# Layer 2 of a two-layer kernel: from a scheduler's order to an order laid out by hand

## The chip, the cores and the metric

The kernel runs on one core of one Trainium2 chip. The metric is the device time of one execution in microseconds (us), lower is better. Every number below comes from the times of the kernel before, from the page of its one profiled execution, or from an answer of that execution's trace.

## The reference

An input of 4 images, 192 channels, 128 x 128 pixels, passes through two residual layers, `x = x + layer(GroupNorm(x))`. Layer 1 (fractional and ordinary Fourier transforms) is not touched. Layer 2 is a selective scan over the 16384 pixels of each image, with 384 inner channels and 16 states per channel, all in float32. Cut to what matters:

```python
seq = layernorm_over_channels(groupnorm(x))            # 192 channels
xs, z = split(in_proj_w @ seq)                         # 384 + 384
u = silu(causal_conv4(xs))
dt, B, C = split(x_proj_w @ u, [12, 28])               # 12 + 16 + 16 rows
dt = softplus(dt_proj_w @ dt + b)
# for each pixel t, channel d, state s:
h[d, s] = h[d, s] * exp(dt[d] * A[d, s]) + (dt[d] * u[d]) * B[s]
y[d] = sum_s h[d, s] * C[s] + u[d] * Dp[d]
out = x + out_proj_w @ (y * silu(z))
```

## The kernel before, in words

Layer 1 (`layer0` in the code) ends before layer 2 (`layer1`) begins; the first scan of layer 2 starts at 2670.8 us of the profiled execution. Layer 2 works on chunks of T = 512 pixels, 32 for each image, 128 in all. The inner channels lie on partitions as NJ = 3 tiles of 128; the states go in pairs (G = 2), so a chunk has 3 x 8 = 24 groups, one for each tile j and pair of states.

**The front of a chunk** (`front`, a generator that stops at each `yield`): load `xm` (L557), GroupNorm on DVE (L560), mean over channels by matmuls with ones (L566), subtraction (L568), square on ACT (L572), variance by matmuls (L578), square root on ACT (L583), reciprocal and a diagonal matrix on DVE (L584, L586), its broadcast by matmuls (L589), scaling (L593); then in_proj (L606) to `xs` (L612), the convolution as four matmuls with diagonal matrices (L617), silu to `u` (L620) and, of the other half of in_proj, to `zs` (L622); x_proj (L628), copied to `xd` (L632), whose rows of B and C go to DRAM as `dbc`; dt_proj (L640), softplus to `dt` (L643) and the product `dtu = dt * u` on DVE (L644).

**A group** (`inputs`, `decays`, `scans`): `bc` is a pair's B and C, broadcast from DRAM to all partitions (1 MB per load). `db = dtu * B` is made on DVE from `dp`, a copy of `dtu` in PSUM (L677), or, for one group of three, on POOL from `dtu` itself (L675). ACT makes two `da = exp(dt * A)` in PSUM (L687). DVE runs two scans `h` (L701), ACT copies their last column to `carry` (L705), POOL multiplies `hc = h * C` (L707), PE adds up `hc` in PSUM by matmuls with the identity (L712), and after a tile's last pair adds `u * Dp` (L714). DVE then gates, `yg = py * zs` (L716). `finish` makes out_proj (L727), adds `xm` (L731) and stores. A float32 matmul is two PE instructions in the trace.

**What sets the order.** The groups go in two halves of states, each over the three tiles (`HALVES = 2`). `bc` has 6 buffers of the 8 that a chunk needs, `da` two PSUM banks, `ps` (all of the front's matmuls and `finish`) two, each `py{j}` one of its own, `h` four, `hc` three. The loop at the end of `layer1` asks for `inputs` two groups ahead, `decays` one ahead and a step of the next chunk's `front` at every second group; what is left of it is asked for at group 21. The order in which instructions then stand in each engine's queue is not this one: the tile framework's scheduler lays it out when the program is built. Each engine works through its own queue in that order, and waits on semaphores for the other engines, for DMAs and for buffers to come free.

Of the kernel before, what the change touches and what calls it, by code (L numbers as in the profile page):

```python
# [19 lines left out]
CH = 96  # L20
# [462 lines left out]
def layer1(tc, xmid, out, st2, w, n_tok=S * S):  # L483
# [5 lines left out]
    with ExitStack() as ctx:  # L489
# [7 lines left out]
        fp = pool("l1f", 2)  # L497
        jp = pool("l1j", 5)
        tp = pool("l1t", 2)
        bcp = pool("l1b", 6)  # L500
# [4 lines left out]
        psa = pool("l1a", 2, space=PSUM)  # L505
        psy = pool("l1y", 1, space=PSUM)
# [15 lines left out]
        nc.vector.memset(eps, 1e-5)  # L522

# [22 lines left out]

        last = {}
# [4 lines left out]
        def front(i, got):  # L552

            b, ch = divmod(i, NCHUNK)
            at = slice(ch * T, (ch + 1) * T)
            xm = xp.tile([CH, 2, T], F32, name="xm")
            nc.sync.dma_start(out=xm, in_=xmid[b][:, at].rearrange("(t p) f -> p t f", p=CH))  # L557
            s = lp.tile([CH, 2, T], F32, name="s")
            for t in range(2):
                nc.vector.tensor_scalar(  # L560
                    s[:, t, :], xm[:, t, :], st2[:, b, t, 0:1], st2[:, b, t, 1:2],
                    ALU.subtract, ALU.mult,
                )
            mu = psum()
# [5 lines left out]
            )  # L570
            sq = lp.tile([CH, 2, T], F32, name="sq")
# [4 lines left out]
            for q in range(4):  # L576
                for t in range(2):
                    nc.tensor.matmul(  # L578
                        var[:, q : q + 1], sq[:, t, q * 128 : (q + 1) * 128], ones[0:CH, 0:1],
                        start=t == 0, stop=t == 1,  # L580
                    )
            rs = tp.tile([128, 4], F32, name="rs")
            nc.scalar.activation(rs, var[:, 0:4], AF.Sqrt, bias=eps, scale=1.0 / C)  # L583
            nc.vector.reciprocal(rs, rs)  # L584
            dg = lp.tile([128, 4, 128], F32, name="dg")
            nc.vector.tensor_tensor(dg, _bc(ident, 1, 4), _bc(rs, 2, 128), ALU.mult)  # L586
            rb = psum()
# [6 lines left out]
            xs = fp.tile([128, NJ, T + 3], F32, name="xs")  # L594
            if ch == 0:
                nc.gpsimd.memset(xs[:, :, 0:3], 0.0)
            else:
                nc.gpsimd.tensor_copy(xs[:, :, 0:3], last["xs"][:, :, T : T + 3])
            last["xs"] = xs
            zs = [jp.tile([128, T], F32, name="zs") for _ in range(NJ)]  # L600
            u = [jp.tile([128, T], F32, name="u") for _ in range(NJ)]
# [8 lines left out]

            for j in range(NJ):
                nc.scalar.activation(xs[:, j, 3:], in_proj(j), AF.Identity, bias=bxz[:, j : j + 1])  # L612
            yield
            for j in range(NJ):
                pc = psum()
                for k in range(4):
                    nc.tensor.matmul(  # L617
                        pc, dcw[:, j, k, :], xs[:, j, k : k + T], start=k == 0, stop=k == 3
                    )
                nc.scalar.activation(u[j], pc, AF.Silu, bias=cb[:, j : j + 1])  # L620
            for j in range(NJ):
                nc.scalar.activation(  # L622
                    zs[j], in_proj(NJ + j), AF.Silu, bias=bxz[:, NJ + j : NJ + j + 1]
                )
            yield
            px = psum()
            for j in range(NJ):
                nc.tensor.matmul(  # L628
                    px[0 : RANK + 2 * NS], xpT[:, j, :], u[j], start=j == 0, stop=j == NJ - 1
                )  # L630
            xd = tp.tile([RANK + 2 * NS, T], F32, name="xd")
            nc.scalar.copy(xd, px[0 : RANK + 2 * NS])  # L632
            dbc = dram.tile([2, NS, T], F32, name="dbc")
            nc.sync.dma_start(out=dbc.rearrange("a s t -> (a s) t"), in_=xd[RANK:, :])
            yield
            dt = [jp.tile([128, T], F32, name="dt") for _ in range(NJ)]
            dtu = [jp.tile([128, T], F32, name="dtu") for _ in range(NJ)]
            for j in range(NJ):
# [3 lines left out]
                )  # L642
                nc.scalar.activation(dt[j], pd, AF.Softplus, bias=dtb[:, j : j + 1])  # L643
                nc.vector.tensor_mul(dtu[j], dt[j], u[j])  # L644
            yield
            got.update(xm=xm, zs=zs, u=u, dt=dt, dtu=dtu, dbc=dbc)

        HALVES = 2  # L650
        NG = NS // G // HALVES
        groups = [(hf, j, hf * NG + q) for hf in range(HALVES) for j in range(NJ) for q in range(NG)]
        NGR = len(groups)

        def load_bc(i, got):

            sg = len(got["bc"])
            t = bcp.tile([128, 2, G, T], F32, name="bc")
            nc.sync.dma_start(
                out=t, in_=got["dbc"][:, sg * G : (sg + 1) * G, :].partition_broadcast(128)  # L660
            )
            got["bc"].append(t)

        def inputs(n, k, got):

            hf, j, sg = groups[k]
            if k % NG == 0:
                dp = psd.tile([128, T], F32, name="dp")
                nc.scalar.copy(dp, got["dtu"][j])  # L669
                got["dp"] = dp  # L670
            if sg == len(got["bc"]):
                load_bc(n, got)
            db = scp.tile([128, G, T], F32, name="db")
            if k % 3 == 2:
                nc.gpsimd.tensor_tensor(db, _bc(got["dtu"][j], 1, G), got["bc"][sg][:, 0], ALU.mult)  # L675
            else:
                nc.vector.tensor_tensor(db, _bc(got["dp"], 1, G), got["bc"][sg][:, 0], ALU.mult)  # L677
            got["db", k] = db

        def decays(n, k, got):  # L680

            hf, j, sg = groups[k]
            das = []
            for g in range(G):
                st = sg * G + g
                da = psa.tile([128, T], F32, name="da")
                nc.scalar.activation(da, got["dt"][j], AF.Exp, scale=A[:, j, st : st + 1])  # L687
                das.append(da)
            got["da", k] = das

        def scans(n, k, got):
            hf, j, sg = groups[k]
            ch = n % NCHUNK
            if k == 0:
                got["carry"] = tp.tile([128, NJ, NS], F32, name="carry")
                got["before"], last["carry"] = last.get("carry"), got["carry"]
            db, das = got.pop(("db", k)), got.pop(("da", k))
            h = scp.tile([128, G, T], F32, name="h")
            for g in range(G):
                st = sg * G + g  # L700
                nc.vector.tensor_tensor_scan(  # L701
                    h[:, g, :], das[g], db[:, g, :],
                    0.0 if ch == 0 else got["before"][:, j, st : st + 1], ALU.mult, ALU.add,
                )
            nc.scalar.copy(got["carry"][:, j, sg * G : (sg + 1) * G], h[:, :, T - 1])  # L705
            hc = scp.tile([128, G, T], F32, name="hc", bufs=3)
            nc.gpsimd.tensor_tensor(hc, h, got["bc"][sg][:, 1], ALU.mult)  # L707
            if hf == 0 and k % NG == 0:
                got["py", j] = psy.tile([128, T], F32, name=f"py{j}")
            py = got["py", j]  # L710
            for g in range(G):
                nc.tensor.matmul(py, ident, hc[:, g, :], start=sg == 0 and g == 0, stop=False)  # L712
            if hf == HALVES - 1 and k % NG == NG - 1:
                nc.tensor.matmul(py, ddp[:, j, :], got["u"][j], start=False, stop=True)  # L714
                yg = op.tile([128, T], F32, name="yg", bufs=4)
# [176 lines left out]
```

## Time and profile before

| what | us or share |
|---|---|
| median of 3 runs | 15999.61 (15998.29 to 16002.89) |
| the profiled execution's own time | 15985.05 |
| its span, first to last instruction | 15983.3 |
| PE, busy share of the span | 85% |
| DVE | 78% |
| POOL | 62% |
| ACT | 58% |
| DMA queue of all tensor transfers, share of 16 engines | 27.1% |
| ACT table loads of layer 2, per chunk (L687, L620, L643, L622, L583) | 16 |

The page gives for each engine its busy time, then groups of instructions by line: engine, operation, written tile and read tiles, shapes, count, busy time, mean ns of one, and the engine's idle time just before them with the engine that ended it. Shares of the whole span mix the two layers: layer 2 is about five sixths of it. The time of the profiled execution lies 14.6 us under the median.

### The profile page before, as it was taken

The page shows a single profiled execution, that of the slowest core. Times are in us where ns is not written, and L with a number is a line of the kernel's source. Part 1 is how long each engine was busy: PE and PEld are TensorE (multiplying, and loading weights), DVE is VectorE, ACT ScalarE, POOL GpSimd, SP SyncE. Part 2 cuts the span into 40 slices and gives each one's busy share as a digit, 9 for nine tenths or more (in the row PEclk, how much of TensorE's full clock was granted, in tenths as well). Part 3 has the DMA queues.
Part 4 walks back from the last instruction along what each step waited for, and adds up shares of the span by engine and source line. Part 5 has one row for each costly group of instructions (what it writes and reads, how often), then busy time and mean ns, then how long its engine had stood idle before and what let it go on. Part 6 is the DMA issues. An engine that isn't in the chain of part 4 may idle for free. (4 is left out here: it accounts for less than half of the span.)

```text
span 15983.3 us, 106086 instructions
## 1 busy us (share of the span) xinstructions
PE 13547.5 (85%) x31224; PEld 5507.4 (34%) x31224; DVE 12438.0 (78%) x11315; ACT 9233.8 (58%) x14682; POOL 9838.8 (62%) x4338
## 2 busy tenths in 40 slices
PE   6978978888888888888888888888888888888888
PEld 5342432333333333333333333333333333333333
DVE  5345244888888888888888888888888888888888
ACT  1122123666666666666666666666666666666665
POOL 0000002777777777777777777777777777777777
PEclk8566566999999999999999999999999999999999
DMA  5344322222222222222222222222222222222222
GB/s 154 92 113 115 91 80 81 88 81 93 93 88 93 88 81 92 93 88 93 90 84 87 93 92 89 92 84 85 93 93 88 93 91 81 89 93 88 93 91 76
DMA packets 488164, 1462.09 MB, mean 91 GB/s; under 512 B 63805, under 2 KB 114750, under 8 KB 487070
## 3 DMA queue, kind: packets, MB, share of 16 engines
q1 hardware_dynamic: 474270, 1404.97, 27.1%
q0 software_dynamic: 13312, 50.34, 1.0%
q8 instruction: 246, 4.03, 0.1%
q14 instruction: 336, 2.75, 0.1%
HBM read 1312.45 MB, written 142.74 MB: 91 GB/s over the span
## 5 line engine op out<-in xcount | busy, mean ns | idle before, releaser
L707 POOL TENSOR_TENSOR hc<-h,bc 128x1024 f32<-128x1024 f32 x3072 | 7344.9, 2397 | 3547.8 <-DVE h L701 2869.2
L701 DVE TENSOR_TENSOR_SCAN h<-da,carry,db 128x512 f32<-128x512 f32 x5952 | 7294.2, 1264 | 891.4 <-ACT da L687 891.0
L712 PE MATMUL py<-hc,ident 128*128 128x512 f32 x12288 | 6353.3, 644 | 1768.2 <-POOL hc L707 1767.7
L687 ACT ACTIVATE da<-dt,c_A_log 128x512 f32<-128x512 f32 x6144 | 4216.6, 690 | 3715.3 <-DVE h L701 3658.7
L712 PEld LDWEIGHTS py<-hc,ident 128*128 128x128 f32 x12288 | 2287.4, 199 | 5318.4 <-POOL hc L707 2872.6
L677 DVE TENSOR_TENSOR db<-dp,bc 128x1024 f32<-128x1024 f32 x2048 | 2448.6, 1200 | 393.9 <-DMA bc<-dbc 388.9
L675 POOL TENSOR_TENSOR db<-dtu,bc 128x1024 f32<-128x1024 f32 x1024 | 2450.3, 2393 | 36.4 <-DMA bc<-dbc 36.0
L606 PE MATMUL ps<-s,c_wiT 96*128 96x512 f32 x3072 | 1454.0, 602 | 69.3 <-ACT u L620 48.1
L617 PE MATMUL ps<-xs,dcw 128*128 128x512 f32 x3072 | 1373.9, 596 | 115.8 <-ACT u L620 115.8
L687 ACT ACT_TABLE_LOAD x1018 | 1306.1, 1283 | 16.3
L463 POOL DMA_DIRECT2D xmid<-xt x64 | 40.6, 634 | 1528.4 <-DVE xt L461 1528.4
L606 PEld LDWEIGHTS ps<-s,c_wiT 96*128 96x128 f32 x3072 | 572.5, 193 | 926.8 <-issue 616.2
L617 PEld LDWEIGHTS ps<-xs,dcw 128*128 128x128 f32 x3072 | 571.2, 189 | 897.2 <-issue 676.9
L461 DVE TENSOR_TENSOR xt<-xt,pr 96x1024 f32<-96x1024 f32 x128 | 155.8, 1217 | 784.3 <-PE pr L458 784.3
L727 PE MATMUL ps<-yg,c_woT 128*96 128x512 f32 x1536 | 701.7, 592 | 0.0
L644 DVE TENSOR_TENSOR dtu<-dt,u 128x512 f32<-128x512 f32 x384 | 656.5, 1736 | 35.5 <-ACT dt L643 30.0
L452 ACT COPY x<-ps 16x512 f32<-16x512 f32 x128 | 73.5, 574 | 828.3 <-PE ps L449 828.3
L705 ACT COPY carry<-h 128x2 f32<-128x2 f32 x3072 | 548.3, 178 | 1.5 <-DVE h L701 1.5
L669 ACT COPY dp<-dtu 128x512 f32<-128x512 f32 x768 | 447.3, 582 | 96.0 <-DVE db L677 96.0
L620 ACT ACT_TABLE_LOAD x382 | 490.1, 1283 | 9.4 <-PE ps L617 2.8
L628 PE MATMUL ps<-u,c_xpT 128*44 128x512 f32 x768 | 484.6, 782 | 9.0 <-ACT u L620 9.0
L192 DVE TENSOR_SCALAR xn<-xt,gst 96x1024 f32<-96x1024 f32 x256 | 199.6, 803 | 373.4 <-PE ps L260 330.2
(158 smaller groups left out, 10543.5 us busy)
## 6 DMA issues: line engine op xcount, KB each, us to landing
bc<-dbc SPq DMA_DIRECT2D x1024, 1024.0 KB, 5.5
xt<-in_x SPq DMA_DIRECT2D x192, 768.0 KB, 5.0
xmid<-xt POOLq DMA_DIRECT2D x64, 768.0 KB, 4.7
xm<-xmid SPq DMA_DIRECT2D x128, 384.0 KB, 4.3
out<-o SPq DMA_DIRECT2D x128, 384.0 KB, 3.1
df<-u SPq DMA_DIRECT2D x16, 512.0 KB, 2.7
u<-df SPq DMA_DIRECT2D x16, 512.0 KB, 5.0
dimg<-img SPq DMA_DIRECT2D x4, 2048.0 KB, 9.5
```

What stands on the lines that cost most here:

```text
L606: nc.tensor.matmul(pp, wiT[:, t, m * 128 : (m + 1) * 128], s[:, t, :], start=t == 0, stop=t == 1)
L617: nc.tensor.matmul(pc, dcw[:, j, k, :], xs[:, j, k : k + T], start=k == 0, stop=k == 3)
L620: nc.scalar.activation(u[j], pc, AF.Silu, bias=cb[:, j : j + 1])
L644: nc.vector.tensor_mul(dtu[j], dt[j], u[j])
L675: nc.gpsimd.tensor_tensor(db, _bc(got["dtu"][j], 1, G), got["bc"][sg][:, 0], ALU.mult)
L677: nc.vector.tensor_tensor(db, _bc(got["dp"], 1, G), got["bc"][sg][:, 0], ALU.mult)
L687: nc.scalar.activation(da, got["dt"][j], AF.Exp, scale=A[:, j, st : st + 1])
L701: nc.vector.tensor_tensor_scan(h[:, g, :], das[g], db[:, g, :], 0.0 if ch == 0 else got["before"][:, j, st : st + 1], ALU.mult, ALU.add,)
L705: nc.scalar.copy(got["carry"][:, j, sg * G : (sg + 1) * G], h[:, :, T - 1])
L707: nc.gpsimd.tensor_tensor(hc, h, got["bc"][sg][:, 1], ALU.mult)
L712: nc.tensor.matmul(py, ident, hc[:, g, :], start=sg == 0 and g == 0, stop=False)
L727: nc.tensor.matmul(po[0:CH], woT[:, j, t * CH : (t + 1) * CH], got["yg", j], start=j == 0, stop=j == NJ - 1,)
```

## The change

Only layer 2 changes, in ten points:

1. The whole of it is issued inside `tc.manual_schedule()`: instructions stand in every engine's queue in the order in which the program text issues them.
2. `HALVES` is gone: the groups of a chunk go tile by tile, k = 8 j + (pair of states). `bc` has 8 buffers, so that all B and C of a chunk stay resident; the load of a pair for the next chunk is issued when its buffer's last reader of this chunk has been issued: pairs 0 to 6 in iterations 17 to 23, pair 7 in iteration 0 of the next chunk. `dp` is copied 3 times a chunk, not 6.
3. GroupNorm is two `activation(Identity, scale, bias)` on ACT, with a bias tensor `nmr` made once, in place of two `tensor_scalar` on DVE.
4. Silu and softplus are issued in pairs where two inputs are there: u(0) with u(1), u(2) with z(0), softplus 0 with 1, softplus 2 alone, z(1) with z(2).
5. POOL makes `db` in two groups of five (10 of 24), not one of three (8 of 24).
6. `da` has 3 PSUM banks, not 2; an exponential is issued right after each scan, for the state 3 places on. `py` has 2 banks shared by the three tiles, not one for each.
7. PE's sums for a group are issued one iteration after its scans. The gate of tile j is issued an iteration later still.
8. `front` has 22 steps, not 7 or so, one for each iteration. It starts at iteration 22 of two chunks before: in iteration k stands step k+3 of the next chunk (var in 2, the root in 3, `rs` and `dg` in 4, in_proj 0 to 2 in 7 to 9, conv 0 to 2 in 10 to 12, silu_u(0), silu_u(1) in 12, silu_u(2) and silu_z(0) in 14, `xd` in 15, softplus and `dtu` 0 and 1 in 17, 2 in 18, silu_z(1) and (2) in 19).
9. `finish` is three steps, in iterations 3, 4 and 5 of the next chunk.
10. The last three columns of `xs` go to a tile `halo` of their own, so one `xs` buffer is enough; `h` has 3 buffers, not 4; `xm` is loaded earlier.

In each iteration the text issues: `inputs` two groups ahead, the two scans with an exponential after each, `carry`, `hc`, the sums of the group before, the gate, `finish`, a step of `front`, and loads. The diff, cut to its core:

```diff
-        bcp = pool("l1b", 6)
+        bcp = pool("l1b", NS // G)
-        psa = pool("l1a", 2, space=PSUM)
-        psy = pool("l1y", 1, space=PSUM)
+        psa = pool("l1a", 3, space=PSUM)
+        psy = pool("l1y", 2, space=PSUM)
...
             for t in range(2):
-                nc.vector.tensor_scalar(
-                    s[:, t, :], xm[:, t, :], st2[:, b, t, 0:1], st2[:, b, t, 1:2],
-                    ALU.subtract, ALU.mult,
-                )
+                nc.scalar.activation(
+                    s[:, t, :], xm[:, t, :], AF.Identity,
+                    bias=nmr[:, b, t : t + 1], scale=st2[:, b, t, 1:2],
+                )
...
+            a = conv(0)
+            yield
+            c = conv(1)
+            yield
+            silu_u(0, a)
+            silu_u(1, c)
+            a = conv(2)
+            yield
+            c = in_proj(NJ)
+            yield
+            silu_u(2, a)
+            silu_z(0, c)
             px = psum()
...
+            def softplus(j, pd):
                 nc.scalar.activation(dt[j], pd, AF.Softplus, bias=dtb[:, j : j + 1])
                 nc.vector.tensor_mul(dtu[j], dt[j], u[j])
...
+            a, c = dt_proj(0), dt_proj(1)
+            yield
+            softplus(0, a)
+            softplus(1, c)
+            a = dt_proj(2)
+            yield
+            softplus(2, a)
+            a, c = in_proj(NJ + 1), in_proj(NJ + 2)
+            yield
+            silu_z(1, a)
+            silu_z(2, c)
...
-            if k % 3 == 2:
+            if 2 * k % 5 < 2:
...
+        with tc.manual_schedule():
...
+            for pos, (n, k) in enumerate(order):
+                j, sg = divmod(k, NG)
+                if pos + 2 < len(order):
+                    inputs(*order[pos + 2])
+                scans(pos, n, k)
+                if pos:
+                    sums(*order[pos - 1])
+
+                if sg == 1 and pos > 1:
+                    m, q = order[pos - 2]
+                    gate(m, q // NG)
+                    if q == NGR - 1:
+                        tail = finish(m)
+                if k in (3, 4, 5):
+                    next(tail, None)
+                if k == NGR - 2:
+                    for _ in ahead:
+                        pass
+                    ahead = front(n + 2) if n + 2 < total else iter(())
+                next(ahead, None)
+                if k == NGR - 8 and n + 2 < total:
+                    load_x(n + 2)
+                if k >= NGR - 7 and n + 1 < total:
+                    load_bc(n + 1, k - (NGR - 7))
+                if k == 0 and n:
+                    load_bc(n, NG - 1)
```

`scans` after the change issues, for each of its two states, a scan and then `decay`, the exponential three states on:

```python
            for q in range(G):
                st = sg * G + q
                nc.vector.tensor_tensor_scan(
                    h[:, q, :], das.pop(G * pos + q), db[:, q, :],
                    0.0 if ch == 0 else g["before"][:, j, st : st + 1], ALU.mult, ALU.add,
                )
                decay(G * pos + q + 3)
            nc.scalar.copy(g["carry"][:, j, sg * G : (sg + 1) * G], h[:, :, T - 1])
            hc = scp.tile([128, G, T], F32, name="hc", bufs=3)
            nc.gpsimd.tensor_tensor(hc, h, g["bc", sg][:, 1], ALU.mult)
            g["hc", k] = hc
```

## The prediction

> **What bounds the kernel now.** I read the page first, for the engines and the costliest groups.
>
> ```profile
> span 15983.3 us, 106086 instructions
> ...
> L707 POOL TENSOR_TENSOR hc<-h,bc 128x1024 f32<-128x1024 f32 x3072 | 7344.9, 2397 | 3547.8 <-DVE h L701 2869.2
> L701 DVE TENSOR_TENSOR_SCAN h<-da,carry,db 128x512 f32<-128x512 f32 x5952 | 7294.2, 1264 | 891.4 <-ACT da L687 891.0
> L712 PE MATMUL py<-hc,ident 128*128 128x512 f32 x12288 | 6353.3, 644 | 1768.2 <-POOL hc L707 1767.7
> ...
> L677 DVE TENSOR_TENSOR db<-dp,bc 128x1024 f32<-128x1024 f32 x2048 | 2448.6, 1200 | 393.9 <-DMA bc<-dbc 388.9
> ...
> L628 PE MATMUL ps<-u,c_xpT 128*44 128x512 f32 x768 | 484.6, 782 | 9.0 <-ACT u L620 9.0
> L644 DVE TENSOR_TENSOR dtu<-dt,u 128x512 f32<-128x512 f32 x384 | 656.5, 1736 | 35.5 <-ACT dt L643 30.0
> ```
>
> All of these are layer 2. By the timeline its first scan starts at 2670.8, so a chunk takes (15983.3-2670.8)/128 = 104.0 us. The busy times over that stretch:
>
> ```profile
> 2670.80:15983.30 13312.50, 11343.68 (x25764) 4543.17 (x25764) 11355.22 (x9971) 8726.00 (x13918) 9740.89 (x4222) 0.95 0.26 89
> ```
>
> The columns after the length are PE, PEld, DVE, ACT and POOL: PE and DVE are both busy 85%, POOL 73%, ACT 66%, DMA 26%. No engine is full; DVE idles about 15 us of each chunk. The table of waits, then one chunk's timeline of DVE and of ACT, say where.
>
> ```profile
> DVE h L701 <- ACT da L687: 928.2, 559, 3.4
> DVE db L677 <- DMA bc<-dbc: 388.9, 126, 4.9
> DVE s L593 <- PE ps L589: 356.8, 127, 3.2
> ```
>
> ```profile
> 9066.52 3.62 DVE L701 TENSOR_TENSOR_SCAN h<-da,carry,db 128x512 f32<-128x512 f32 x3
> 9073.81 1.23 DVE L677 TENSOR_TENSOR db<-dp,bc 128x1024 f32<-128x1024 f32 x1 [3.67 <-DMA bc<-dbc]
> ...
> 9081.34 2.46 DVE L701 TENSOR_TENSOR_SCAN h<-da,carry,db 128x512 f32<-128x512 f32 x2 [2.25 <-ACT da L687]
> 9086.05 1.28 DVE L701 TENSOR_TENSOR_SCAN h<-da,carry,db 128x512 f32<-128x512 f32 x1 [2.25 <-ACT da L687]
> ```
>
> ```profile
> 9077.32 1.28 ACT L622 ACT_TABLE_LOAD   x1
> 9078.62 0.69 ACT L622 ACTIVATE zs<-ps,bxz 128x512 f32<-128x512 f32 x1
> 9079.32 1.28 ACT L687 ACT_TABLE_LOAD   x1
> 9080.62 0.69 ACT L687 ACTIVATE da<-dt,c_A_log 128x512 f32<-128x512 f32 x1
> ```
>
> A silu between two exponentials holds the scan for two table loads. PE's timeline gives its rate, warm and cold:
>
> ```profile
> 9062.73 7.03 PE L617 MATMUL ps<-xs,dcw 128*128 128x512 f32 x16
> 9103.71 4.83 PE L628 MATMUL ps<-u,c_xpT 128*44 128x512 f32 x6
> ```
>
> Sixteen take 7.03, so one starts each 0.43 us; the six of L628 need 0.8 each after idle gaps (2.77 for six in the chunk before).
>
> **What the Trainium skill says.** "ScalarE: Activation LUTs", Table sets: functions of different sets need a load at each change. The trace agrees, at 1283 ns. "SBUF — State Buffer", Who interferes with whom: a DVE instruction with two SBUF inputs and a GpSimd one that reads SBUF exclude each other for a whole instruction. The trace agrees: `dtu` takes 1.74 us in the mean where `yg`, as large but with a PSUM input, takes 0.67. "TensorE: Matmul & The Clock Gate", Part 1: the array's clock halves after an idle window of some 3.4 us; L628 above fits.
>
> **The change part by part.** Prices are start to start in the timelines: scan 1.18, DVE `db` 1.12, `hc` 2.33, POOL `db` 2.36, exponential 0.63, table load 1.29, 512-wide PE pass 0.43.
>
> *DVE work.* GroupNorm leaves it: 2 x 1.22 = 2.4 less. POOL makes 10 `db` instead of 8: 2 x 1.12 = 2.2 less. What stays: 48 x 1.18 + 14 x 1.12 = 72.3; the two mean/scale steps, `rs`, `dg`, three gates, two adds 6.1; three `dtu` 2.0 plus 2.3 for one lock by a POOL `db`. Sum **82.7 us**.
> *POOL*: 24 x 2.33 + 10 x 2.36 + 0.4 = 79.9. *PE*, unchanged: 178 passes x 0.43 + 3 for the small ones = 79.5. *ACT*: 12 table loads instead of 16 (-5.1), 3 `dp` copies instead of 6 (-1.7), 2 GroupNorm steps (+1.4, priced as `xs` at 0.68: the same operation on as many columns; the trace has no such step reading SBUF, so 0.6 to 1.1 each, `sq`'s 1.06 for 1024 columns being the top; beside the scans in iteration 22, and 1.4 on the path if ACT has no lead there): 68 becomes 63. DMA: the same eight 1 MB loads; eight buffers put each one 5 groups (16 us) ahead against 5.5 us to landing, so the DMA wait goes (-3 us); In SP's queue the loads stand behind `dbc`'s store (1.6 us to landing) and the `xm` load, neither of which comes late; if they did, 3 us return. POOL's halo copy (0.2) waits for xs(2) of ACT, which is done before `hc` of that iteration. A third `da` bank gives the exponentials one scan more of lead, 1.4 us beyond what they need; silu pairs cost 3.9.
>
> So the three engines lie within 4% of each other and each now runs in a fixed order. What is late next has to be followed by hand. I take the steady chunk from iteration 7 (DVE free at 0, POOL at 3.1) and let each instruction start when its queue and inputs allow:
> - *7 to 12*: PE must do 10 pieces, sums, three in_proj and two conv, 21.5 us without a gap from 3.1; conv(1) ends at 24.6. DVE is through group 12 at 19.3. ACT's table is loaded at 21.4, but silu_u(1) waits for conv(1): silu ends 25.6, table 26.8, two exponentials, carry, and only then the `dp` copy, ending 28.8. DVE's next instruction at 21.6 is db(16), which needs it: **7.2** idle, the largest.
>   DVE's ends of groups 7 to 14 on this clock: 3.5, 5.8, 10.0, 13.4, 15.8, 19.3, 21.6, 32.3.
> - *14 to 16*: silu_u(2) with silu_z(0) holds one exponential: 0.9.
> - *17, 18*: `dtu` stands in DVE's queue before the next scans and waits for softplus behind a table load: 2.3 and 2.9. Behind them in DVE's queue are the next `db` and both scans, so `hc` and ACT's exponentials wait too. Before, scans filled that (0.4 idle at L644). In 18 PE's in_proj for silu_z(2) waits 4.3 for softplus(2) to free its bank, with the next sums behind it; PE has by then caught up, so it costs nothing if `hc` keeps two buffers free, else up to 4.
> - *19 to 22*: silu_z pair: 0.9.
> - *20 to 4*: POOL never pauses (13 instructions, 30.4 us); PE's sums, var and po0 follow it, so gate and the first add wait 0.4 and 2.5.
>
> Idle sum 17.0, near the 15 of before: the DMA and exponential stalls go, the fixed order's come. 82.7 + 17.0 is 99.7; the clock kept by hand closes at 100.2. Clock: L628's excess is 6 x (0.782-0.593) = 1.1 us a chunk; somewhere between 0 and that also falls on PE's chain after, take 0.5. **100.7 us**. Saving 104.0-100.7 = 3.3, x 127 steady chunks = 419 us. Prologue and layer 1 unchanged within 10 us. 15985-419 = 15566 for the profiled execution, which lay 15 below the median: **15580**. Adding a PE latency of 0.15 to every hand-over on the first chain, or losing the lock, moves a chunk by 2 either way: 15330 to 15830.
>
> **The rivals.**
> 1. *The waits are covered and DVE's work is the bound.* If PE's block of 7 to 12 starts earlier, 2.8 of the 7.2 goes, and if POOL's run doesn't hold the adds, 2.9 more; with the lock's 2.3 the chunk is 92.2: 11.8 x 127 = 1500, **14500**. For it: POOL has 20 us of slack a chunk. Against: POOL, PE and DVE must all recover within three `hc` buffers.
> 2. *PE goes cold in the block of 7 to 12.* After idle gaps (iterations 18 to 22 leave some of 3 to 4 us) the pass takes 0.85. The block is on the path, so from 3.3 us more, a pass at 0.50, it is slower than before; with half the block cold, +10.7 to 111.4: +7.4 x 127 + 16000 = **16940**. Against: conv passes run at 0.43 in the trace, and the block is dense.
> 3. *No difference*: the fixed order is not what runs, or idle rises to 20 and eats the saved work: **16000**. Against the first: the built order has 12 table loads a chunk and silu in pairs.
>
> **How the numbers follow.** Forecast 0.72, rival 1 0.11, rival 2 0.12, rival 3 0.05. A difference under 0.2% (32 us) can't be told from none. Faster 0.83, same 0.05, slower 0.12. The range leaves out rival 2's 16940 (0.12) and most of rival 1, and takes in the forecast's bounds, half the road to rival 1 and the case of no change: 15050 to 16010.
>
> **What would show it.** Right: chunk near 100.7; one DVE idle of about 7 us before db(16), put down to ACT's `dp`, whose ACT queue waited for conv; 2 to 3 us before each `dtu`; no wait for `bc`; DVE busy near 82%; POOL without pause in groups 20 to 4. Wrong: the db(16) gap missing (rival 1), or conv passes above 0.5 us (rival 2), or `hc` stopped by PE's sums.

## The result and the profile after

The changed kernel takes **16221.27 us** (median of 4 runs, 16200.8 to 16230.14); the kernel before, beside it on the same chip, 16001.25 (15998.29 to 16023.56). The ratio is 1.0133, 95% interval 1.0115 to 1.015: slower by 1.3%, about 220 us. The forecast was 15580 with a range of 15050 to 16010, so sign and range were both missed.

The profiled execution took 16200.8, its span 16199.0. First the page of the kernel after, with the rows that answer to those of before (line, engine, operation, tiles, count | busy us, mean ns | idle of the engine just before, and what ended it):

```profile
span 16199.0 us, 103417 instructions
...
L756 POOL TENSOR_TENSOR hc<-h,bc 128x1024 f32<-128x1024 f32 x3072 | 7196.7, 2356 | 3359.9 <-DVE h L749 3329.6
L767 PE MATMUL py<-hc,ident 128*128 128x512 f32 x12288 | 6449.1, 653 | 1732.5 <-POOL hc L756 1722.8
L749 DVE TENSOR_TENSOR_SCAN h<-da,carry,db 128x512 f32<-128x512 f32 x5952 | 7220.8, 1261 | 197.7 <-ACT da L736 197.1
...
L723 DVE TENSOR_TENSOR db<-dp,bc 128x1024 f32<-128x1024 f32 x1792 | 2157.3, 1204 | 903.2 <-ACT dp L718 902.3
L622 PE MATMUL ps<-s,c_wiT 96*128 96x512 f32 x3072 | 1687.1, 677 | 384.4 <-ACT dt L689 383.0
L641 PE MATMUL ps<-xs,dcw 128*128 128x512 f32 x3072 | 1381.0, 592 | 0.0
...
L690 DVE TENSOR_TENSOR dtu<-dt,u 128x512 f32<-128x512 f32 x384 | 513.4, 1362 | 671.0 <-ACT dt L689 670.9
...
L587 DVE SCALAR_TENSOR_TENSOR s<-ps,s 96x1024 f32<-96x1024 f32 x128 | 156.2, 1221 | 559.4 <-PE ps L585 559.4
```

The scans' wait for exponentials fell from 891 us to 197, and DVE's wait for `bc` is gone. In their place stand waits that were small or absent: `db` for the `dp` copy (902), `dtu` for softplus (671), and one that the prediction did not have at all: **559 us before the subtraction of the mean (L587), which waits for PE's `mu` matmuls (L585).**

The same stretch of layer 2 after, from 11 us ahead of its first scan on (length, then PE, PEld, DVE, ACT, POOL busy, the granted clock, DMA share, GB/s):

```profile
2660.00:16199.00 13539.00, 11395.08 (x25776) 4680.43 (x25776) 10728.86 (x9466) 8023.76 (x13288) 10160.83 (x4606) 0.93 0.26 88
```

By chunk (divided by 128): DVE works 83.8 us and idles (13539.0 - 10728.9)/128 = 22.0. Before it worked 88.7 and idled 15.3. The change took away 4.9 us of work and put 6.7 us of idle time in. That is 1.8 a chunk, times 127 = 225 us: the whole difference of 220, within the rounding. The table of waits of DVE from 2700 us on (us in total, times, longest) says what the idle time waits for:

```profile
DVE db L723 <- ACT dp L718: 896.0, 128, 7.6
DVE dtu L690 <- ACT dt L689: 644.3, 254, 2.9
DVE s L587 <- PE ps L585: 556.1, 126, 6.1
DVE o L788 <- PE ps L783: 247.3, 127, 3.1
DVE yg L774 <- PE py L769: 229.7, 131, 3.2
DVE h L749 <- ACT da L736: 204.9, 254, 1.0
```

One chunk in DVE's timeline shows them one after the other (start, length, operation, count, and in brackets the idle time before it and what ended it):

```profile
8013.03 1.22 DVE L723 TENSOR_TENSOR db<-dp,bc 128x1024 f32<-128x1024 f32 x1 [7.03 <-ACT dp L718]
...
8022.08 1.28 DVE L749 TENSOR_TENSOR_SCAN h<-da,carry,db 128x512 f32<-128x512 f32 x1 [0.80 <-ACT da L736]
...
8029.72 3.35 DVE L690 TENSOR_TENSOR dtu<-dt,u 128x512 f32<-128x512 f32 x2 [2.21 <-ACT dt L689]
...
8038.30 0.69 DVE L690 TENSOR_TENSOR dtu<-dt,u 128x512 f32<-128x512 f32 x1 [2.87 <-ACT dt L689]
...
8056.10 2.44 DVE L749 TENSOR_TENSOR_SCAN h<-da,carry,db 128x512 f32<-128x512 f32 x2
8063.25 1.22 DVE L587 SCALAR_TENSOR_TENSOR s<-ps,s 96x1024 f32<-96x1024 f32 x1 [4.71 <-PE ps L585]
```

The last two lines are what the forecast lacked. DVE is through its scans at 8058.54 and has more to do, but L587 stands next in its queue. POOL's and PE's timelines of the same time say why `mu` is late:

```profile
8048.45 2.38 POOL L721 TENSOR_TENSOR db<-dtu,bc 128x1024 f32<-128x1024 f32 x1
8050.78 2.36 POOL L756 TENSOR_TENSOR hc<-h,bc 128x1024 f32<-128x1024 f32 x1
8053.08 2.37 POOL L721 TENSOR_TENSOR db<-dtu,bc 128x1024 f32<-128x1024 f32 x1
8055.40 6.97 POOL L756 TENSOR_TENSOR hc<-h,bc 128x1024 f32<-128x1024 f32 x3
```

```profile
8053.19 1.98 PE L767 MATMUL py<-hc,ident 128*128 128x512 f32 x4 [2.67 <-POOL hc L756]
8057.82 3.06 PE L767 MATMUL py<-hc,ident 128*128 128x512 f32 x4 [2.64 <-POOL hc L756]
8060.67 2.54 PE L585 MATMUL ps<-s,ones 96*96 96x512 f32 x4
```

A number in brackets is the group of the chunk: hc(22) is `hc` of group 22. The scans of group 22 end at 8051.5, but POOL is late: it is still in hc(21), which stood behind db(23), and has db(0) of the next chunk to do as well. hc(22), the first of the three in the last line, starts at 8055.40 and ends at 8057.73. PE's sums of group 22 start then; the `mu` matmuls, which need only `s` (made by ACT at 8052.33 to 8053.9), stand behind these sums in PE's queue and end at 8063.2; then DVE goes on. The Trainium skill ("TensorE: Matmul & The Clock Gate", Part 2) says that PE keeps matmuls in program order, and the trace agrees: `mu` was ready to run from 8053.9 on and PE stood idle for 2.64 us before 8057.82, without taking it. That nothing else held `mu` back is what the first experiment shows.

### The profile page after: what moved, and what is told of

It is laid out like the page before. It is cut to its first block, busy times and chain, and to the rows that moved or that the text cites. A ratio compares the mean times of both kernels' runs of the same rounds, so it can differ in the third digit from the quotient of the medians.

```text
span 16199.0 us, 103417 instructions
## 1 busy us (share of the span) xinstructions
PE 13599.8 (84%) x31224; PEld 5647.6 (35%) x31224; DVE 11807.0 (73%) x10804; ACT 8524.8 (53%) x14045; POOL 10258.8 (63%) x4722
## 4 chain that ended last, share of the span: by engine, by line
PE 32%; DVE 29%; issue 15%; POOL 13%; ACT 9%; DMA 1%; POOLq 0%; SPq 0%; DVEq 0%; ACTq 0%
DVE h L749 17%; PE py L767 12%; POOL hc L756 10%; PE ps L641 5%; DVE db L723 5%; PE ps L622 5%; ACT da L736 3%; POOL db L721 3%; DVE dtu L690 3%; PE ps L783 2%; ACT L689 2%; PE ps L585 2%; PE ps L260 1%; DVE dg L608 1%; ACT dt L689 1%
## 5 line engine op out<-in xcount | busy, mean ns | idle before, releaser
L756 POOL TENSOR_TENSOR hc<-h,bc 128x1024 f32<-128x1024 f32 x3072 | 7196.7, 2356 | 3359.9 <-DVE h L749 3329.6
L767 PE MATMUL py<-hc,ident 128*128 128x512 f32 x12288 | 6449.1, 653 | 1732.5 <-POOL hc L756 1722.8
L721 POOL TENSOR_TENSOR db<-dtu,bc 128x1024 f32<-128x1024 f32 x1280 | 3046.2, 2380 | 23.1 <-DMA bc<-dbc 23.1
L723 DVE TENSOR_TENSOR db<-dp,bc 128x1024 f32<-128x1024 f32 x1792 | 2157.3, 1204 | 903.2 <-ACT dp L718 902.3
L622 PE MATMUL ps<-s,c_wiT 96*128 96x512 f32 x3072 | 1687.1, 677 | 384.4 <-ACT dt L689 383.0
L641 PE MATMUL ps<-xs,dcw 128*128 128x512 f32 x3072 | 1381.0, 592 | 0.0
L622 PEld LDWEIGHTS ps<-s,c_wiT 96*128 96x128 f32 x3072 | 662.9, 220 | 1311.5 <-issue 746.9
L690 DVE TENSOR_TENSOR dtu<-dt,u 128x512 f32<-128x512 f32 x384 | 513.4, 1362 | 671.0 <-ACT dt L689 670.9
L641 PEld LDWEIGHTS ps<-xs,dcw 128*128 128x128 f32 x3072 | 581.6, 189 | 736.9 <-issue 736.9
L587 DVE SCALAR_TENSOR_TENSOR s<-ps,s 96x1024 f32<-96x1024 f32 x128 | 156.2, 1221 | 559.4 <-PE ps L585 559.4
L635 ACT ACTIVATE xs<-ps,bxz 128x512 f32<-128x512 f32 x384 | 264.4, 688 | 550.7 <-PE ps L622 475.0
L458 PE MATMUL pr<-cat,c_w2T 48*96 48x512 f32 x512 | 473.6, 1079 | 3.1 <-ACT cat L455 3.1
L449 PE MATMUL ps<-xn,c_w1T 96*16 96x512 f32 x512 | 475.3, 1034 | 0.0
```

Source lines behind the costliest of these rows:

```text
L622: nc.tensor.matmul(pp, wiT[:, t, m * 128 : (m + 1) * 128], s[:, t, :], start=t == 0, stop=t == 1)
L641: nc.tensor.matmul(pc, dcw[:, j, k, :], xs[:, j, k : k + T], start=k == 0, stop=k == 3)
L721: nc.gpsimd.tensor_tensor(db, _bc(g["dtu"][j], 1, G), g["bc", sg][:, 0], ALU.mult)
L723: nc.vector.tensor_tensor(db, _bc(g["dp"], 1, G), g["bc", sg][:, 0], ALU.mult)
L756: nc.gpsimd.tensor_tensor(hc, h, g["bc", sg][:, 1], ALU.mult)
L767: nc.tensor.matmul(py, ident, hc[:, q, :], start=sg == 0 and q == 0, stop=False)
```

## The experiments

My **theory** after the result: the time is lost to the laid-out order itself, by instructions that stand in a queue ahead of work that could go on, and the step that I missed is the one chain POOL `hc` - PE sums - `mu` - DVE. **Rivals**: PE's lower clock after short idle gaps; POOL's two extra `db`; GroupNorm on ACT; or a fault common to any order. Edits are against the changed kernel unless another is named. The middle two columns of this table are us from 2700 us of the profiled execution to 15 us before its end. Gains "a chunk" are differences of medians, divided by 128.

| kernel | median us | DVE busy | DVE idle | ratio to before, 95% |
|---|---|---|---|---|
| after | 16221.27 | 10698 | 2786 | 1.0133 (1.0115-1.015) |
| mu_first | 15931.1 | 10633 | 2622 | 0.9957 (0.9943-0.9972) |
| dp_early | 15835.69 | 10690 | 2432 | 0.9901 (0.9887-0.9916) |
| dtu_late | 15786.8 | 10944 | 2110 | 0.9871 (0.9856-0.9885) |
| three | 14972.03 | 10707 | 1548 | 0.9364 (0.9348-0.9379) |
| free_order | 15570.66 | 11033 | 1829 | 0.9737 (0.9723-0.9752) |
| pool_third | 16396.1 | 10906 | 2757 | 1.0251 (1.0199-1.0303) |
| warm | 16183.07 | 10670 | 2768 | 1.0117 (1.0102-1.0132) |
| norm_dve | 16362.54 | 11242 | 2421 | 1.0222 (1.0208-1.0236) |
| norm_act_alone | 15932.0 | 10993 | 2222 | 0.9951 (0.9939-0.9964) |
| five | 14737.23 | 10822 | 1200 | 0.9214 (0.9199-0.923) |
| six | 14590.55 | 11012 | 857 | 0.9116 (0.9104-0.9129) |
| seven | 14876.47 | 11221 | 946 | 0.9292 (0.9278-0.9306) |
| front_first | 15372.29 | 10648 | 2011 | 0.9603 (0.9587-0.9619) |
| front_gate | 15688.26 | 10862 | 2093 | 0.98 (0.9785-0.9815) |

### mu_first: the `mu` matmuls ahead of the sums, nothing else

```diff
+                if k == NGR - 1:
+                    next(ahead, None)
                 if pos:
                     sums(*order[pos - 1])
...
-                next(ahead, None)
+                if k != NGR - 1:
+                    next(ahead, None)
```

> Edit: in iteration 23 the two mean matmuls (mu, L585) are issued ahead of PE's sums for group 22; nothing else moves. Theory (one late chain: DVE's L587 stands ahead of the scans of the next group and waits for mu, mu stands behind sums(22), sums(22) waits for hc(22), hc(22) stands behind two db on POOL): the wait before L587, 4.4 us a chunk after the change, falls under 1, and 3 to 4 us of it come off the chunk, as POOL stands idle 2.4 and 1.7 us just after it: 105.7 to about 102, 15,750 us. Rival (POOL and PE are full there, so another wait takes its place, at the first add, the gate or the scan's buffer): under 1.5 us a chunk, above 16,030 us.

Measured: 15931.1, 290 us or 2.3 a chunk less than after, between theory and rival. DVE's waits of this kernel:

```profile
DVE o L788 <- PE ps L783: 582.1, 127, 7.5
...
DVE s L587 <- PE ps L585: 0.7, 3, 0.3
```

The wait for `mu` is gone as expected, but the add of the last chunk's output (L788), which waits for out_proj, grew from 247 to 582. out_proj and `var` also stand behind sums in PE's queue, so most of the time won was waited for a little later: the theory holds for this wait, but it is one of several on the same chain. Some 0.7 of the 2.3 is not this wait at all: `dg` (L608) took 909 ns in the mean here, 1621 after the change (more on this at the end).

### dp_early: the third `dp` copied two iterations sooner, ahead of the silu pair

```diff
-            if sg == 0:
-                g["dp"] = psd.tile([128, T], F32, name="dp")
-                nc.scalar.copy(g["dp"], g["dtu"][j])
+            if sg == 0 and k != 2 * NG:
+                copy_dp(n, j)
...
+                if k == 2 * NG - 4:
+                    copy_dp(n, 2)
```

> Edit: the dp copy of the third tile is issued in iteration 12, ahead of the silu pair on ACT, not in 14 behind it. Theory (db(16) waits only because the copy stands behind silu_u(1), which waits for conv(1)): the wait of db(16), 7.05 us a chunk, goes; some 3.5 us of it come back as a wait of the second scan of group 14 for its exponential, which stands behind the same pair; net 3.5 us, 15,780 us. Rival (the whole stall belongs to the silu pair and the copy is only where it shows): the scans wait as long, gain under 1 us a chunk, above 16,090 us.

Measured: 15835.69, 3.0 a chunk less than after; the theory's figure is 56 us away. The wait of 896 before `db` is gone; the scans' wait for exponentials behind the silu pair rose from 205 to 887.8:

```profile
DVE h L752 <- ACT da L739: 887.8, 381, 4.1
```

The silu pair still waits for conv(1), and that now shows at the scans; but DVE and POOL get on with `db` and scans before it, and DVE's whole idle time falls by 354 us. The total fits better than its parts: 5.3 a chunk came back at the scans, not the 3.5 of the theory, and the waits before `dtu` and for `mu` fell by 1.1 and 0.9, which it did not have.

### dtu_late: the product `dtu` one iteration after its softplus

```diff
             def softplus(j, pd):
                 nc.scalar.activation(dt[j], pd, AF.Softplus, bias=dtb[:, j : j + 1])
+
+            def product(j):
                 nc.vector.tensor_mul(dtu[j], dt[j], u[j])
...
             a = dt_proj(2)
             yield
+            product(0)
+            product(1)
             softplus(2, a)
...
             yield
+            product(2)
             silu_z(1, a)
```

> Edit: each product dtu is issued one iteration after its softplus, so that a db and two scans stand before it in DVE's queue. Theory: the waits before dtu, 5.2 us a chunk, fall under 1; 3 to 4 us come off the chunk, the rest comes back as scans waiting for exponentials behind the softplus table loads; POOL's idle of 3.7 and 4.7 us after them gives the room: 15,780 us. Rival (ACT's table loads bound this stretch anyway): all of it comes back before the scans, above 16,090 us.

Measured: 15786.8, 3.4 a chunk less than after, in the theory's range. All of the 644 before `dtu` is gone; `mu` (563.8) and `db` (895.5) are unchanged. DVE worked longer, since `dtu` now meets POOL more often (2095 ns in the mean, not 1362): what came back did so as work, and not as the wait for exponentials that the theory named, which fell from 205 to 128.

### three: these three edits together

> Edit: the three edits together. Theory (DVE's idle is the loss, and PE, POOL and ACT have room): the gains add up to 10 to 11 us a chunk, chunk about 95, 14,870 us, faster than both kernels. Rival (PE's 80 to 89 us and POOL's 80 us a chunk, in bursts that don't coincide, bound it near 100): the gains don't add up, above 15,500 us.

Measured: 14972.03, 1249 us or 9.8 a chunk less than after; the three alone add up to 8.7, so they don't eat each other's gain. The theory's figure was 102 us lower. It is 6.4% faster than before. DVE's waits of this kernel:

```profile
DVE h L757 <- ACT da L744: 815.5, 381, 4.1
DVE yg L782 <- PE py L777: 392.7, 300, 3.9
DVE o L796 <- PE ps L791: 289.8, 128, 4.2
DVE s L587 <- PE ps L585: 29.5, 45, 2.1
```

The chunk is now (14969.2 - 2671)/128 = 96.1 us. PE's idle time over the stretch of the table fell from 2129 us to 1645, and the granted clock of layer 2 rose from 0.93 to 0.99, with no edit to PE's work.

### free_order: the same text, with the order left to the scheduler

```diff
-        with tc.manual_schedule():
+        if True:
```

> Edit: the kernel after the change, with the same program text, but not under manual_schedule: the scheduler lays out the queues again. Theory (the other parts of the change save DVE work and the fixed order then loses it in waits): the scheduler moves other work in front of waiting instructions, the waits before db(16), dtu and L587 shrink from 16.7 to under 6 us a chunk, chunk 95 to 100: 14,800 to 15,400 us. Rival (the buffers and the pairs lose it, whoever lays out the order): within 1% of the kernel after, 16,050 to 16,380 us.

Measured: 15570.66, 5.1 a chunk less than after, but 170 us above the theory's range. The waits of this kernel:

```profile
DVE h L749 <- POOL hc L756: 1401.6, 323, 5.5
DVE db L723 <- ACT dp L718: 217.6, 127, 3.1
```

The waits of the laid-out order go (`mu` and the adds altogether, `db` from 896 to 218, `dtu` from 644 to 62), and another comes: 1402 us in which a scan waits for POOL's `hc` to free an `h` buffer, of which the change left three. In the laid-out order three are enough: its table of waits has no such row. So the laid-out order is what made the kernel slow, and the rest of the change with the scheduler's order is 2.6% faster than before. Why the scheduler lets POOL fall behind was not followed further.

### pool_third: POOL makes `db` for 8 groups, as before

```diff
-            if 2 * k % 5 < 2:
+            if k % 3 == 2:
```

> Edit: in the kernel after the change, POOL makes one db in three again (8 of 24), so one and not two stand ahead of hc(22). Theory (the wait for mu comes of POOL's two db ahead of hc(22)): the wait before L587 falls by about 2.4 from 4.4 us a chunk, and DVE gets 2.2 us more work: about the same time, 16,100 to 16,300 us. Rival (the wait before L587 is PE's cold clock and place in the queue alone): the wait stays above 3.8, and 2.2 us a chunk come on top: 16,500 us.

Measured: 16396.1 (16280.38 to 16498.09, so the interval is wide), slower than after and above the theory's 16,300. The wait for `mu` fell from 556 to 241, as it should if POOL's two `db` make it late, but the add's wait rose from 247 to 563, and DVE had 208 us more to do. Giving the two back moves the wait, it doesn't remove it.

### warm: PE kept busy in its idle gaps

```diff
+                if k in (NGR - 5, NGR - 4, NGR - 3, NGR - 2):
+                    nc.tensor.matmul(
+                        psum(), ident, dcw[:, 0].rearrange("p k c -> p (k c)"), start=True, stop=True
+                    )
```

> Edit: in the kernel after the change, one extra 512-wide float32 matmul (0.86 us, two passes) of constants into a spare ps bank in each of iterations 19 to 22, where PE stands idle 1.5 to 3 us at a time; its product is not used. Theory (of the 4.7 us before L587, 1.8 are the passes of sums(22) and mu at half clock after those idle times): the granted clock rises above 0.95, the wait before L587 falls by 1 to 2 us a chunk: 15,980 to 16,100 us. Rival (the clock plays no part, and more PE work only delays): no gain, 16,220 to 16,330 us.

Measured: 16183.07, 38 us less than after, between theory and rival; the granted clock of layer 2 rose only from 0.93 to 0.94. The `mu` passes ran at 600 ns in the mean, as in the kernel before, instead of 662, and the waits changed so:

```profile
L585 PE MATMUL ps<-s,ones 96*96 96x512 f32 x512 | 244.6, 600 | 8.2 <-ACT s L578 8.2
DVE o L788 <- PE ps L783: 492.1, 129, 5.9
DVE s L587 <- PE ps L585: 387.3, 127, 3.2
```

The wait for `mu` lost 1.3 of its 4.4 a chunk: that is what the filled gaps, and with them the clock, had in it. The rest, 3.0, stays with `mu` as fast as in the kernel before: it is the queue. The add took back 1.9. The rival "low clock" is real as a part, and not the cause.

### norm_dve and norm_act_alone: where GroupNorm runs

The first puts GroupNorm back on DVE in the changed kernel; the second makes this one part of the change alone, in the kernel before.

```diff
-                nc.scalar.activation(
-                    s[:, t, :], xm[:, t, :], AF.Identity,
-                    bias=nmr[:, b, t : t + 1], scale=st2[:, b, t, 1:2],
+                nc.vector.tensor_scalar(
+                    s[:, t, :], xm[:, t, :], st2[:, b, t, 0:1], st2[:, b, t, 1:2],
+                    ALU.subtract, ALU.mult,
                 )
```

> Edit: the kernel after the change with GroupNorm back on DVE as two tensor_scalar; all else as after. Theory (DVE's work counts in full where it doesn't lie in one of DVE's waits, and a tensor_scalar on SBUF is locked out by POOL): +1.2 to 3.0 us a chunk, 16,370 to 16,600 us. Rival (it goes into the wait before L587 or another, being issued in iteration 22 just ahead of it): within 0.5 us a chunk, 16,160 to 16,285 us.

> Edit: the kernel before, with only GroupNorm moved to ScalarE (one part of the change alone, in the scheduler's order). Theory (DVE's work is on the path): 2.4 us a chunk less, 15,650 to 15,750 us. Rival (ACT's two steps, 1.4 us, go in front of exponentials that the scans wait for in this order, with two da banks): within 0.7 us a chunk of before, 15,910 to 16,090 us.

Measured: norm_dve 16362.54, 141 us or 1.1 a chunk more than after, just under the theory's range. DVE has 544 us more to do (4.3 a chunk), since GroupNorm's two instructions take 2216 ns each where they stand here, beside POOL's `hc` and `db`, not 1221 as in the kernel before, and it idles 365 less: `mu` waits 109, not 556, because DVE arrives later; the add waits 440, not 247. norm_act_alone 15932.0, 79 us or 0.6 a chunk less than the runs of before beside it, in the rival's range. There DVE's work falls by 335 us (2.6 a chunk), and the scans' wait for exponentials rises from 928 to 1187.6 (2.0 a chunk):

```profile
DVE h L705 <- ACT da L691: 1187.6, 781, 4.3
```

Both ways GroupNorm on ACT is a gain, but only about a quarter of the work that it takes off DVE (0.6 of 2.6, 1.1 of 4.3). Row L578 of norm_dve:

```profile
L578 DVE TENSOR_SCALAR s<-xm,st 96x512 f32<-96x512 f32 x256 | 557.7, 2216 | 0.0
```

### five and six: PE's front work ahead of its sums

`five` is `three` with the front's matmuls of more iterations ahead of the sums, out_proj ahead of them too, and each gate one iteration later; `six` adds `var` (iteration 2):

```diff
+        FIRST = (2, 7, 8, 9, 10, 11, 13, NGR - 1)     # five: without the 2
...
+                if k in (3, 4, 5):
+                    next(tail, None)
+                if k in FIRST:
+                    next(ahead, None)
                 if pos:
                     sums(*order[pos - 1])
...
-                if sg == 1 and pos > 1:
-                    m, q = order[pos - 2]
+                if sg == 2 and pos > 2:
+                    m, q = order[pos - 3]
```

> Edit: on top of the three edits together, the front's matmuls of iterations 7 to 11 and 13 and the out_proj matmuls are issued ahead of the sums, and each gate one iteration later. Theory (what is left of DVE's idle, 12 us a chunk, is again PE's matmuls standing behind sums that wait for hc): the waits before yg and o (5.4 us) fall under 1.5 and the wait for exponentials (6.4 us) under 4; chunk 96.1 to about 90 to 92: 14,250 to 14,500 us. Rival (POOL's 80 and PE's 80 us a chunk begin to bind): above 14,800 us.

> Edit: on top of five, the variance matmuls of iteration 2 are also issued ahead of the sums. Theory (the first add, 3.6 us a chunk of wait in five, waits for out_proj behind var behind sums that follow POOL's run): the wait falls under 1.8, chunk 94.3 to about 92.5, 14,500 us. Rival (POOL's run of groups 20 to 4 sets the pace there): within 0.5 us a chunk, above 14,670 us.

Measured: five 14737.23, 1.8 a chunk less than three, but above the theory's range: the add still waits 457.6, for out_proj comes after a `var` that is behind the sums. With `var` moved too, six takes **14590.55, 8.8% less than before**, the fastest kernel of the study. That is 1.1 a chunk less than five, between theory and rival. DVE's waits of `six`:

```profile
DVE h L757 <- ACT da L744: 566.9, 508, 2.9
DVE o L796 <- PE ps L791: 122.8, 111, 2.1
```

In all, 857 us idle are left, 6.7 a chunk, against 22 in the changed kernel.

### seven: another choice of POOL's groups

```diff
-            if 2 * k % 5 < 2:
+            if k in (0, 5, 8, 10, 12, 13, 15, 17, 18, 20):
```

> Edit: on top of six, POOL makes db in groups 0, 5, 8, 10, 12, 13, 15, 17, 18, 20 in place of 0, 3, 5, 8, 10, 13, 15, 18, 20, 23: still 10, but two fewer in its unbroken run of groups 20 to 4. Theory (that run's 30 us hold DVE there): 1 to 2 us a chunk less than six, 14,250 to 14,400 us. Rival (PE's block of 7 to 14 binds as much, and POOL's two db now fall into it): no gain or a loss, above 14,480 us.

Measured, on top of six: 14876.47, slower by 286, as the rival had it. `o` waits less (39.7) but scans now wait 458.1 for a `db` that POOL makes too late.

### front_first and front_gate: only the missed chain

`front_first` takes the changed kernel and puts `mu`, `var` and out_proj ahead of the sums; `dp`, `dtu` and the gates stay. `front_gate` adds the gates one iteration later (edits as in five, with `FIRST = (2, NGR - 1)`).

> Edit: the kernel after the change with mu, var and out_proj (iterations 23, 2, and 3 and 4) issued ahead of the sums of those iterations; the waits of db(16) and dtu stay as they are. Theory (the term that the forecast missed is one chain, hc to sums to mu, var, out_proj, and all of it comes off once none of the three stands behind the sums): the waits before L587 and before the first add are together under 1.5 us a chunk, against 6.3 after the change and 4.6 with mu alone; the chunk loses 5 to 6 us and comes to about the forecast's 100.7: 15,450 to 15,620 us. Rival (POOL's run of groups 20 to 4 takes the time itself): like mu alone, above 15,850 us.

> Edit: on top of that, each gate is issued one iteration later. Theory (the gate's wait, 1.9 us a chunk against 0.4 in the forecast, comes of ddp standing behind late sums): it falls under 0.3, and 1 to 1.6 us a chunk come off: 15,270 to 15,470 us. Rival (the wait goes to the next instruction): within 0.4 us a chunk of the kernel with the three moved.

Measured: front_first 15372.29, 849 us or 6.6 a chunk less than after and 4.0% faster than before, better than the theory's range. Its waits:

```profile
DVE db L723 <- ACT dp L718: 931.9, 128, 8.0
DVE dtu L690 <- ACT dt L689: 644.1, 254, 2.9
...
DVE yg L774 <- PE py L769: 127.6, 141, 2.1
...
DVE o L788 <- PE ps L783: 31.4, 120, 0.7
DVE s L587 <- PE ps L585: 1.5, 6, 0.3
```

The two largest terms that the forecast had right, db(16) and `dtu`, stay; `mu`, the add and half of the gate's wait go. Its chunk is (15373.2 - 2671)/128 = 99.2, near the 100.7 of the forecast. The nearness flatters the forecast a little: front_first also takes away the first add's wait, for which the forecast had 2.5, and without it the forecast would be 98.2. With this said, what the forecast lacked was this one chain through PE's queue. front_gate 15688.26 is slower than front_first by 316, against both expectations. The gate's wait is gone as meant, but `dg` (L608), a DVE instruction with both inputs in SBUF, rose from 931 to 3073 ns (2.1 a chunk), and `db` and the add wait 106 and 93 longer. `dg` in front_gate:

```profile
L608 DVE TENSOR_TENSOR dg<-ident,rs 128x512 f32<-128x512 f32 x128 | 393.4, 3073 | 4.4
```

## Why the prediction was wrong, step by step

All figures are us a chunk (totals of after divided by 128); the numbers in italics are iterations of the loop. The forecast's waits add up to 17.1, where it carried 17.0.

| step of the forecast | forecast | measured in after |
|---|---|---|
| *7 to 12*: db(16) waits for `dp` | 7.2 | 7.0 |
| *17, 18*: the two `dtu` | 5.2 | 5.1 |
| *14 to 16*, *19 to 22*: exponentials behind silu | 1.8 | 1.5 |
| *20 to 4*: the first add | 2.5 | 2.0 |
| *20 to 4*: gate | 0.4 | 1.9 |
| *20 to 4*: the subtraction of the mean, L587 | none | **4.4** |
| DVE work | 82.7 | 83.8 |
| clock, and closing of the hand clock | 1.0 | within the rows above |
| chunk | 100.7 | 105.7 |

**What held.** The largest idle time, its place and its chain: ACT's timeline of after has the table load, silu_u(0), 2.60 us of waiting for conv (L641), silu_u(1), another table load, two exponentials, carry and only then the copy:

```profile
8004.52 1.28 ACT L650 ACT_TABLE_LOAD   x1
8005.81 0.69 ACT L650 ACTIVATE u<-ps,c_cb 128x512 f32<-128x512 f32 x1
8009.10 0.69 ACT L650 ACTIVATE u<-ps,c_cb 128x512 f32<-128x512 f32 x1 [2.60 <-PE ps L641]
8009.81 1.28 ACT L736 ACT_TABLE_LOAD   x1
8011.10 1.30 ACT L736 ACTIVATE da<-dt,c_A_log 128x512 f32<-128x512 f32 x2
8012.34 0.18 ACT L754 COPY carry<-h 128x2 f32<-128x2 f32 x1
8012.42 0.58 ACT L718 COPY dp<-dtu 128x512 f32<-128x512 f32 x1
```

The two `dtu` waits (2.21 and 2.87 for 2.3 and 2.9), the 0.80s before scans, and that the wait for `bc` goes, were right too. DVE's busy share of layer 2 is 79%, where 82 was forecast.

**What failed** is the step "*20 to 4*: POOL never pauses (13 instructions, 30.4 us); PE's sums, var and po0 follow it, so gate and the first add wait 0.4 and 2.5". (`po0` is the first half of out_proj.) It saw that PE follows POOL and charged this to `var`, out_proj and the gate, but left out the front instruction that comes first in the same row: `mu`, in iteration 23, behind the sums of group 22. The wait for it, put at nothing, measured 4.4. The forecast's own prices, from the measured end of hc(22) on, find most of it: hc(22) ends at 8057.73, four sums and four `mu` passes at 0.43 are 3.4, and with DVE free at 8058.54 that is a wait of some 2.6 before any lower clock. The run `warm` measured 3.0 with `mu` at the speed of the kernel before, after 4.4. As the idle time stops DVE, POOL gets no `h` either: the "without pause" of the forecast is broken by two idle times of 2.37 and 1.72 after L587.

**Mis-sized terms.** The gate: 1.9 for 0.4, on the same chain. `dg`: priced at 0.74, measured 1.62 (0.9 of the 1.1 by which DVE's work was under-stated), since POOL's work meets it here more often (last section). The clock: 0.5 was set aside for all of PE; the wait for `mu` alone lost 1.3 when the gaps were filled (`warm`). With 4.4 for `mu`, 1.5 for the gate and 1.1 for the work, less 0.3 for the exponentials, 0.5 for the add, 0.2 for db(16), 0.1 for `dtu` and the 1.0 of clock and closing, the sum is 4.9 of the 5.0 between 100.7 and 105.7.

**The rivals.** Rival 3 had the right sign for idle time ("idle rises to 20 and eats the saved work") with no place for it, and it went 1.3% further. Rival 2 looked for the low clock in the block of 7 to 12; the conv passes there ran at 592 ns in the mean, where before had 596 (a pass's own length; the 0.43 of the prediction is from start to start), so it was wrong in its place. The low clock came elsewhere: at `mu`, and in in_proj (L622, 677 ns where before had 602), after 3.04 us in which PE waited for softplus to free a bank. That wait was in the forecast as 4.3 and costless; `dtu_late` and `three` don't tell apart what it cost. Rival 1's 14500 was a matter of the order after all: `six`, with the same instructions on every engine, comes within 0.6% of it, though with 6.7 a chunk of idle time left and not with DVE's work as the bound.

**On balance.** The forecast's mechanism, a saved 4.9 of work against waits of a fixed order, was the right one, and of its five waits all but the gate's were found to 0.5. For the add that is luck: its 2.5 was meant for a chunk without a wait for `mu`, and `mu_first`, which has none, waits 4.5 there (582.1 in all); in after it waits 2.0 because DVE has already waited for the same chain at L587. The sign hung on a margin of 3.3 a chunk that one unlisted wait could take, and the range did not allow for an omission of that kind.

## What to carry to other kernels

When an order is laid out by hand, list for every engine each instruction of another stage that stands behind a late one, and give each of them a time: the first that is left out decides. In a queue that keeps its order, issue what is ready ahead of what waits for another engine (`mu` ahead of the sums), and issue a consumer one step later than its producer (`dtu`); three such edits turned +1.3% into -6.4%, and with the rest of PE's front moved too, -8.8%. When a wait is taken away, look at once for the next on the same chain: `mu_first` gave back more than half of the 4.4 at the add, and moving the gate in `front_gate` cost more than it won.

## What the runs showed of the hardware that was not expected

**One lock can last two instructions.** The Trainium skill ("SBUF — State Buffer", Who interferes with whom) has a DVE instruction with two SBUF inputs and a GpSimd one that reads SBUF exclude each other for a whole instruction. The traces agree that they exclude each other, but DVE's turn doesn't always come when the running POOL instruction ends. In `six`, DVE's and POOL's timelines:

```profile
8084.35 4.34 DVE L608 TENSOR_TENSOR dg<-ident,rs 128x512 f32<-128x512 f32 x1
```

```profile
8083.44 4.70 POOL L764 TENSOR_TENSOR hc<-h,bc 128x1024 f32<-128x1024 f32 x2
```

`dg` became due 0.9 us into the first of two `hc` of 2.35 each, and ended 0.55 after the second. It can take 691 ns (the shortest of each of these kernels); the median of its 128 is 2677 in six, a wait for one POOL instruction, with 4389 as the longest, and 5293 in free_order, a wait for two. Its mean was 739 ns in the kernel before, 1621 in after, 3250 in six and 5007 in free_order, with the same operands each time. It depends on how POOL's queue happens to stand, and so an edit far from it, the gate's in `front_gate`, moved it by 2.1 us a chunk.

**PE lost speed after idle gaps shorter than 3.4 us.** In the chunk shown, four sums took 3.06 us after a gap of 2.64, and four in_proj passes 3.78 after one of 3.04, where 1.88 to 1.98 is usual. The granted clock was 0.64 from 8057.80 to 8060.70 and 0.50 from 8038.30 to 8042.00, and 1.00 from 8047.00 to 8057.80. The length of the last gap alone does not decide: the sums at 8053.19 took the usual 1.98 after a gap of 2.67. The skill ("TensorE: Matmul & The Clock Gate", Part 1) has the clock halve after an idle window of some 3.4 us, a window that runs free and doesn't start with the gap. No gap here is that long, nor was the one of 2.85 us ahead of L628 in the kernel before, where the forecast took the page to fit: the halved rate fits, the window is not shown. Three gaps in a row (1.49, 2.67, 2.64) came before the slow sums, one alone before the slow in_proj passes. What brings the clock down stays open; no run here varied the length of one gap by itself.
